# A graph layer with a fixed gather rhythm: a shorter SyncE program, copied pairs from octet 10 on, x held once in SBUF, and another order for the last octets

## The chip, the core and the metric

The kernel runs on one core of one Trainium2 chip. The core has five engines that work side by side, each through its own list of instructions in order: TensorE (PE in the profile; PEld is its load of weights), VectorE (DVE), ScalarE (ACT), GpSimd (POOL) and SyncE (SP), which only issues DMAs and handles registers. The metric is the device time of one execution in microseconds (us), median of several.

## The reference

There are 12500 nodes with 64 features and 400000 edges, sorted by their target node:

```python
m_in = concatenate([x[src], x[dst], edge_attr], axis=-1)      # 400000 x 144
h = silu(m_in @ W1 + b1)
messages = silu(h @ W2 + b2)
agg = segment_sum(messages, dst, num_segments=12500)
out = layernorm(x + silu(concatenate([x, agg], axis=-1) @ W3 + b3))
```

## The kernel before

**Tiles and octets.** 128 edges are a tile, two tiles a pair, eight tiles an *octet*; there are 3125 tiles and 391 octets (the last has five tiles). The 400000 edges are sorted by target, so the targets of an octet lie in a window of 48 nodes that begins at the target of its first edge (`base`). The loop at line 641 runs over the octets `o` and holds the program of PE, ACT, DVE and SP in an order that is written out by hand; POOL's order is the framework's.

**One octet.** The product of the source rows with W1's first part comes from a table `pa` in HBM that the kernel makes in octets 1 to 7 (`table`, L177). From octet 12 on (`RAW`) POOL gathers rows of `pa`, before that rows of x, one indirect DMA of 128 rows for a tile (`gather`, L373, L382), three octets ahead, into five buffers `ga`. `window_load` (L396) has SP bring the x columns of the octet's window, twice, into `xr`; `window_product` (L404) multiplies them by W1's second part, and `window_copy` (L410) masks the result into `xw`. `load` (L413) has SP bring, for three octets, the targets `dr`, twice 48 partitions, and the attributes into `oh`; `compare_dst` (L426) makes one-hot rows of the targets, `compare_nodes` (L436) one-hot columns `eh`. `first_layer` (L443) adds in PSUM the transposed gathered rows (L462) and one product that brings window and attributes (L466); ACT makes h (L469). `second_layer` (L472) follows two octets later (`SECOND`) and gives m (L484), `add_up` (L487) four octets later (`THIRD`) sums by target, and `add_window` (L496) six octets later (`LAST`) adds the window's 48 sums into `agg`. PE's order within an iteration is: window_product of o+1, first_layer of o, add_up of o-4, second_layer of o-2.

**Tiles that POOL doesn't gather.** Two ways take gathers off POOL.

- *Copied pairs* (`pairs`, L271). x lies transposed in SBUF (`xs`), 64 partitions by nodes, and a second time in partitions 64 to 127. For a copied pair ACT and DVE copy the 256 source columns one by one, 64 partitions by 4 bytes, at a place that a register holds (`columns`, L280; L306 on DVE, L308 on ACT): 72 copies per octet on ACT, in parts of 40 and 32, and 64 on DVE, in four parts of 16 (`RATE` is 136). The list of source nodes comes by `index` (L356), is turned into addresses by `address` (L363), and is loaded into registers at most 16 at a time (L299). Such a pair is multiplied on PE (L465). Copies begin in octet 12, and the first copied pair stands in octet 16.
- *Single rows* (`rows`, L321). From octet 12 on SP loads 16 addresses into registers (L329) and issues 16 DMAs of one `pa` row each (L333) per octet; 256 of them make a pair (`rpairs`, 23 of them).

**The nodes.** While the edges run, nodes whose sums are complete pass in groups of 512 through the second product, layernorm and the store (`node_load`, `node_product`, `node_silu`, `node_stats`, `root`, `inverse`, `divide`, `store`, planned by `todo`). The last two groups come at the end (L728 to L742): their product with x and b3 (`node_product(q, 1)`) stands in iteration NO + 1, the product with agg (`part` 2) behind the last add_window. `limits` (L600, with an iota on POOL, L602) and `verdict` (L615) test whether every target lay in its window; if not, a general path runs instead, which this input doesn't need.

Of the kernel before, what the change touches and what calls it, by code (L numbers as in the profile page):

```python
# [20 lines left out]
P = 128  # L21
# [10 lines left out]
RAW = 12  # L32
TABLES = 7
# [4 lines left out]
XBASE = (0, 64 << 18)  # L38
# [9 lines left out]
@with_exitstack  # L48
def kernel(
    ctx: ExitStack,  # L50
    tc: tile.TileContext,
    x: bass.AP,
    xt: bass.AP,
    src_c: bass.AP,
    src_row: bass.AP,
    dst_c: bass.AP,
    dst_row: bass.AP,
    attr_t: bass.AP,
    dst_2: bass.AP,
    attr_2: bass.AP,  # L60
    base: bass.AP,
    w1: bass.AP,
    b1: bass.AP,
    w2: bass.AP,
    b2: bass.AP,
    w3: bass.AP,
    b3: bass.AP,
    out: bass.AP,
    edges: int,
):  # L70

    nc = tc.nc
    N, D = x.shape

    const = ctx.enter_context(tc.tile_pool(name="const", bufs=1))
    dram = ctx.enter_context(tc.tile_pool(name="dram", bufs=1, space=DRAM))
    pa = dram.tile([N, D], F32, name="pa")
    badi = const.tile([1, 1], I32, name="badi")
    ident = const.tile([P, P], F32, name="ident")  # L90
    make_identity(nc, ident)

    with ExitStack() as inner:
        windows(inner, tc, ident, badi, pa, x, xt, src_c, src_row, dst_c, dst_row, attr_t, dst_2, attr_2, base, w1, b1, w2, b2, w3, b3, out, edges)
# [7 lines left out]
def windows(ctx, tc, ident, badi, pa, x, xt, src_c, src_row, dst_c, dst_row, attr_t, dst_2, attr_2, base, w1, b1, w2, b2, w3, b3, out, edges):  # L102
# [46 lines left out]
    resident(0, 0)  # L149
# [3 lines left out]
    resident(0, XC)  # L153
# [47 lines left out]
    nc.gpsimd.iota(coli, pattern=[[0, 1]], base=0, channel_multiplier=1)  # L201
    colf = fast.tile([P, 2], F32, name="colf")
    nc.vector.tensor_copy(colf[:, 0:1], coli)
    nc.vector.tensor_scalar(colf[:, 1:2], colf[:, 0:1], float(S), None, op0=OP.is_ge)
# [5 lines left out]
    nc.vector.tensor_scalar(colf[:, 1:2], colf[:, 1:2], -float(S), None, op0=OP.mult)  # L210
    nc.vector.tensor_tensor(colf[:, 0:1], colf[:, 0:1], colf[:, 1:2], op=OP.add)
# [8 lines left out]
    nc.vector.tensor_copy(wb, pb)  # L220
    nc.vector.tensor_scalar(wn, pb, colf[:, 0:1], None, op0=OP.add)
# [17 lines left out]
    for k in range(3):  # L239
        t = fast.tile([D + 1, 2, S], F32, name=f"xr{k}")  # L240
        nc.vector.memset(t[D:], 1.0)
        xrs.append(t)
# [13 lines left out]
    with tc.tile_pool(name="gat", bufs=AHEAD + 2) as gat, tc.tile_pool(name="drp", bufs=2) as drp, \  # L256
# [23 lines left out]
        def columns(o, eng, part):  # L280
            if o < RAW:
                return
            lo = (o - RAW) * RATE
            if eng == ENG.Activation:
                lo, n = lo + sum(ACOLS[:part]), ACOLS[part]
            else:
                lo, n = lo + sum(ACOLS) + sum(VCOLS[:part]), VCOLS[part]
            hi, todo = lo + n, n
            while lo < hi:
                j, e0 = lo // (2 * P), lo % (2 * P)  # L290
                if j >= len(pairs):
                    return
                n = min(hi - lo, P - e0 % P, LOADS[lo > hi - todo])
                if pairs[j] not in cols:
                    cols[pairs[j]] = cx.tile([P, P], F32, name="cx")
# [3 lines left out]
                _, regs = nc.values_load_multi_w_load_instructions(  # L299
                    indices[j][0:1, e0:e0 + n], engines=(eng,), min_val=XBASE[s] + XADDR,  # L300
                    max_val=XBASE[s] + XADDR + 4 * (N - 1), skip_runtime_bounds_check_because="src names a node")
                for e, r in zip(range(e0 % P, e0 % P + n), regs):
                    to, frm = t[h, 4 * e:4 * e + 4], xb[h, ds(r - (XBASE[s] + XADDR), 4)]
                    if eng == ENG.DVE:

                        nc.vector.tensor_reduce(to, frm[:, :, None], AX.X, OP.max)  # L306
                    else:
                        nc.scalar.copy(to, frm)  # L308
                lo += n
# [8 lines left out]
        single, rindex = {}, {}  # L318
        pab = pa[:, :].bitcast(U8).rearrange("n d -> (n d)")

        def rows(o):  # L321
            lo = (o - RAW) * ROWS
            j, e0 = lo // (2 * P), lo % (2 * P)
            if o < RAW or j >= len(rpairs):
                return
            if e0 == 0:
                single[rpairs[j]] = rx.tile([P, 2, D], F32, name="rx")
            t = single[rpairs[j]].bitcast(U8)
            _, regs = nc.values_load_multi_w_load_instructions(  # L329
                rindex[j][0:1, e0:e0 + ROWS], engines=(ENG.SP,), min_val=0, max_val=4 * D * (N - 1),  # L330
                skip_runtime_bounds_check_because="src names a node")
            for e, r in zip(range(e0, e0 + ROWS), regs):
                nc.sync.dma_start(t[e % P:e % P + 1, e // P, :], pab[ds(r, 4 * D)].rearrange("(o n) -> o n", o=1))  # L333
# [17 lines left out]
        def begun(o):  # L351

            first, behind = -(-(o - RAW) * RATE // (2 * P)), -(-(o + 1 - RAW) * RATE // (2 * P))
# [16 lines left out]
        winrow, winreg = {}, {}  # L370
        sums = psa.tile([P, 4, S], F32, name="pg")
# [15 lines left out]
        def bases(eng, o):  # L387

            n = min(4, NO - o)
            _, regs = nc.values_load_multi_w_load_instructions(  # L390
                bi[0:1, o:o + n], engines=(eng,), min_val=0, max_val=N - 1,
# [4 lines left out]
        def window_load(o):  # L396
# [3 lines left out]
            frm = xt[:, ds(winreg.pop((ENG.SP, o)), S)]  # L400
            nc.sync.dma_start(xr[:D], frm[:, None, :].to_broadcast([D, 2, S]))
            winrow[o] = xr

        def window_product(o):  # L404
            pw = mis.tile([P, P], F32, name="mm")
            nc.tensor.matmul(pw[:E, :], winrow[o].rearrange("k s w -> k (s w)"), w1bb.rearrange("k s m -> k (s m)"),  # L406
# [6 lines left out]
        def load(c, o0=0, o1=CT // OT):  # L413
# [6 lines left out]
            for k in range(2):  # L420
                nc.sync.dma_start(dr[k * S:(k + 1) * S, e], dst_2[k:k + 1, d].to_broadcast([S, e.stop - e.start]))  # L421
# [21 lines left out]
        def first_layer(o):  # L443
# [6 lines left out]
            if o < RAW:  # L450
                nc.tensor.matmul(p1[:, :k], xw[o % 3], oh, start=True, stop=False, skip_group_check=True)
                pt = mis.tile([P, OT // 2, P], F32, name="mm")
                for i in range(k):
                    nc.tensor.transpose(pt[:, i, :], ga[:, 2 * i:2 * i + 2, :].rearrange("p s d -> p (s d)"), ident)
                xg = msg.tile([P, OT // 2, P], F32, name="m")
                nc.vector.tensor_copy(xg[:, :k], pt[:, :k])
                nc.tensor.matmul(p1[:, :k], w1d, xg[:, :k], start=False, stop=True, skip_group_check=True)
# [163 lines left out]

        for o in range(min(AHEAD, NO)):
            gather(o)
# [14 lines left out]
        with tc.manual_schedule(engines={ENG.PE, ENG.Activation, ENG.DVE, ENG.SP}):  # L638
            compare_dst(0)
            compare_nodes(0)  # L640
            for o in range(NO + THIRD):
# [6 lines left out]
                if o < 2:  # L648
                    for c in parts[2:5] if o == 0 else parts[5:]:
                        resident(0, c)  # L650
# [23 lines left out]
                if o + 1 < NO:  # L674
# [3 lines left out]
                if o >= LAST:  # L678
                    add_window(o - LAST)
# [9 lines left out]
                if o + 1 < NO:  # L689
                    window_copy(o + 1)  # L690
# [16 lines left out]
                if o >= THIRD:  # L707
                    add_up(o - THIRD)
                if 0 <= o - SECOND < NO:
                    second_layer(o - SECOND)  # L710
# [6 lines left out]
                if o == NO - 2:  # L717
# [10 lines left out]
        for o in range(NO + THIRD - LAST, NO):  # L728
            add_window(o)
# [4 lines left out]
        for q in range(rest, NG):  # L734
            node_product(q, 2)
            node_silu(q)
            node_stats(q)
        root(rest, NG)
# [261 lines left out]
```

## Time and profile before

| | us |
|---|---|
| median of 3 runs | 3422.63 |
| lowest and highest | 3420.27 and 3425.53 |
| the profiled execution | 3420.95 |
| its span, first to last instruction | 3418.8 |

Busy time in that span: PE 2283.9, PEld 1545.4, DVE 2433.6, ACT 3109.1, POOL 2542.7 us. In the lines of the profile, L382 is line 382 of the kernel; a group's line reads: line, engine, operation, what it writes <- what it reads, count, then busy time in all, mean ns of one, and the idle time of the engine just ahead of it with what ended it. "issue" means that nothing that the profile shows was waited for. A line of the timeline reads: start, duration, engine, line, operation, tiles, count, and in brackets the idle time before it. SPq and ACTq are an engine's issuing of DMAs and its register work. PEclk is the granted share of TensorE's full clock.

### The profile page before, as it was taken

What the parts mean: (1) busy time and instruction counts of PE and PEld (TensorE: products, weight loads), DVE (VectorE), ACT (ScalarE), POOL (GpSimd) and SP (SyncE); (2) the same over time, 40 slices, a digit from 0 to 9 for tenths busy, and PEclk for the clock granted to TensorE, in tenths of its full rate; (3) what the DMA queues carried; (4) which work ended last, traced back from release to release, by engine and by line L of the source; (5) the groups of instructions that cost most, each with busy time, mean ns of one, the idle gap of its engine ahead of it and who ended that gap; (6) DMA issues with size and microseconds to landing.
All of it is one profiled execution on the core that took longest, in us unless ns stands there. A gap on an engine that the chain in (4) does not pass through costs nothing. (4 is left out here: it accounts for less than half of the span.)

```text
span 3418.8 us, 107012 instructions
## 1 busy us (share of the span) xinstructions
PE 2283.9 (67%) x13764; PEld 1545.4 (45%) x13764; DVE 2433.6 (71%) x26003; ACT 3109.1 (91%) x27413; POOL 2542.7 (74%) x2696
## 2 busy tenths in 40 slices
PE   6777776666666666666666656666667576666667
PEld 4545444444444444444444444434444354444444
DVE  2577777677776777778777777777787776877772
ACT  2499999999999999999999999998999999999992
POOL 7777777777777777777777777776777777777774
PEclk7756566676666777677676667776766766777766
DMA  6532233233333322323332233233223223332322
GB/s 136 119 64 61 62 65 65 62 63 67 69 61 65 66 61 63 68 60 66 72 62 59 62 69 60 62 69 66 62 61 68 61 61 69 65 62 60 69 60 58
DMA packets 202928, 229.05 MB, mean 67 GB/s; under 512 B 133023, under 2 KB 141413, under 8 KB 201301
## 3 DMA queue, kind: packets, MB, share of 16 engines
q1 hardware_dynamic: 101560, 122.63, 16.1%
q0 software_dynamic: 85984, 88.22, 13.8%
q10 hardware_dynamic: 14652, 11.26, 1.5%
q14 instruction: 615, 5.03, 0.5%
q8 instruction: 117, 1.92, 0.2%
HBM read 215.45 MB, written 6.40 MB: 65 GB/s over the span
## 5 line engine op out<-in xcount | busy, mean ns | idle before, releaser
L382 POOL DMA_INDIRECT ga<-pa,sc x2591 | 2449.8, 945 | 813.4 <-issue 702.5
L308 ACT COPY cx<-xs 64x4 uint8 x26568 | 2646.4, 187 | 60.7 <-issue 37.2
L306 DVE TENSOR_REDUCE cx<-xs 64x4 uint8 x23608 | 1684.2, 153 | 527.3 <-issue 477.2
L406 PE MATMUL mm<-w1bb,xr 65*96 65x128 f32 x782 | 234.6, 395 | 839.2 <-DMA xr<-in_xt 673.6
L466 PE MATMUL p<-oh,xw 128*128 128x512 f32 (+1 forms) x758 | 601.7, 890 | 0.0
L480 PE MATMUL p<-w2d,h 128*128 128x128 f32 x3126 | 571.7, 339 | 0.0
L406 PEld LDWEIGHTS mm<-w1bb,xr 65*96 65x96 f32 x782 | 141.0, 226 | 890.3 <-DMA xr<-in_xt 785.1
L493 PEld LDWEIGHTS pg<-eh,m 128*64 128x64 f32 x6250 | 283.0, 175 | 574.6 <-issue 368.2
L480 PEld LDWEIGHTS p<-w2d,h 128*128 128x128 f32 x3126 | 483.1, 236 | 114.7 <-issue 114.7
L493 PE MATMUL pg<-eh,m 128*64 128x48 f32 x6250 | 334.8, 263 | 104.8 <-DVE agg L498 101.8
L433 DVE TENSOR_TENSOR oh<-dr,wrow 96x512 f32<-96x512 int32 x391 | 263.6, 674 | 150.4 <-DMA dr<-in_dst 70.8
L462 PE MATMUL p<-ident,ga 128*128 128x128 f32 x1296 | 318.9, 372 | 68.4 <-DMA ga<-pa,sc 68.1
L469 ACT ACTIVATE h<-p 128x512 f32<-128x512 f32 x391 | 231.7, 592 | 144.8 <-PE p L466 99.9
L462 PEld LDWEIGHTS p<-ident,ga 128*128 128x128 f32 x1296 | 236.1, 196 | 84.6 <-issue 80.3
L484 ACT ACTIVATE m<-p 128x512 f32<-128x512 f32 x391 | 231.4, 592 | 43.5 <-PE p L480 31.2
L439 DVE TENSOR_TENSOR eh<-wrow,dc 128x384 f32<-128x384 f32 x391 | 214.3, 548 | 2.7
L498 DVE TENSOR_TENSOR agg<-agg,pg 128x48 f32 x391 | 78.2, 200 | 188.3 <-PE mm L533 113.3
L466 PEld LDWEIGHTS p<-oh,xw 128*128 128x128 f32 x758 | 179.6, 291 | 0.0
L478 PE MATMUL p<-b2r,one 3*128 3x512 bf16 x391 | 177.5, 454 | 0.0
L411 DVE TENSOR_TENSOR xw<-mm,mask 96x128 f32<-96x128 f32 x391 | 109.6, 280 | 23.1 <-PE mm L406 15.2
L382 POOL DMA_INDIRECT ga<-in_x,sc x96 | 90.8, 946 | 30.2 <-issue 28.0
L465 PE MATMUL p<-cx,w1d 128*128 128x128 f32 x392 | 109.9, 377 | 0.0
(84 smaller groups left out, 780.2 us busy)
## 6 DMA issues: line engine op xcount, KB each, us to landing
rx<-pa SPq DMA_DIRECT2D x5888, 0.2 KB
dr<-in_dst SPq DMA_DIRECT2D x260, 288.0 KB
ga<-pa,sc POOLq DMA_INDIRECT x2591
oh<-in_attr SPq DMA_DIRECT2D x130, 192.0 KB
xr<-in_xt SPq DMA_DIRECT2D x391, 24.0 KB
xs<-in_xt ACTq DMA_DIRECT2D x12, 512.0 KB
cxi<-in_src_row SPq DMA_DIRECT2D x196, 1.0 KB
pa<-v ACTq DMA_DIRECT2D x12, 256.0 KB
```

The lines of the kernel that those rows point to most:

```text
L306: nc.vector.tensor_reduce(to, frm[:, :, None], AX.X, OP.max)
L308: nc.scalar.copy(to, frm)
L382: nc.gpsimd.indirect_dma_start(out=ga[:, i, :], out_offset=None, in_=x if o < RAW else pa[:, :], in_offset=bass.IndirectOffsetOnAxis(ap=sc ...
L406: nc.tensor.matmul(pw[:E, :], winrow[o].rearrange("k s w -> k (s w)"), w1bb.rearrange("k s m -> k (s m)"), start=True, stop=True)
L433: nc.vector.tensor_tensor(oh[:E, :], dr[:, e:e + w], wn[:E, o:o + 1].to_broadcast([E, w]), op=OP.is_equal)
L439: nc.vector.tensor_tensor(eh[:, :n], row[:, None, :].to_broadcast([P, n, S]), rel[:, t0:t0 + n, None].to_broadcast([P, n, S]), op=OP.is_equal)
L462: nc.tensor.matmul(p1[:, i, :], g2.rearrange("p s d -> p (s d)"), ident, is_transpose=True, start=(i == c), stop=False, skip_group_check=True)
L466: nc.tensor.matmul(p1[:, :k], xw[o % 3], oh, start=False, stop=True, skip_group_check=True)
L469: nc.scalar.activation(h[:, :k], p1[:, :k], AF.Silu)
L480: nc.tensor.matmul(p2[:, 2 * i:2 * i + 2, :].rearrange("p s d -> p (s d)"), h[:, i, :], w2d, start=False, stop=(i == k - 1), skip_group_ch ...
L484: nc.scalar.activation(m[:, :n2], p2[:, :n2], AF.Silu)
L493: nc.tensor.matmul(pg[s * D:(s + 1) * D, :], m[:, i, :], eh[:, i, :], start=(i < 2), stop=(i >= n - 2), skip_group_check=True)
```

## The change

- **Slices from doubled columns.** A new array `xt2` holds every column of x's transpose twice in a row. The window's slice is one run of 384 bytes in each of 64 partitions, in place of two of 192. So rows and columns of the two tiles of a pair alternate in `dr`, `mask`, `colf` and `wn` (partition 2w + tile in place of 48 tile + w). The registers of `base` are loaded for SP from a copy times 8 (`bi8`), so that the byte offset needs no step of its own.
- **One DMA for `dr`** in place of two.
- **32 registers at a time** for the single rows, in every second octet.
- **Copies from octet 6 on** (`BEGIN`): copied pairs begin in octet 10.
- **x once.** `xs` is filled in partitions 0 to 63 only; copies for the second tile of a pair read there and write partitions 64 to 127. `address` is one instruction for both tiles.
- **The last octets.** second_layer of the last three octets comes one octet after first_layer; add_up of the last three after two octets and of the three before after three; add_window after 3, 4, 4 and 5. The last window product is made an octet earlier. The two last node groups' first products move from iteration NO + 1 to NO - 3 and NO - 2, `limits` and `verdict` behind the loop, the statistics behind both second products.

```diff
+BEGIN = 6
-XBASE = (0, 64 << 18)
...
-    def resident(s, c):
+    def resident(c):
         w = min(XC, NP - c)
-        nc.scalar.dma_start(xs[s * D:(s + 1) * D, c:c + w], xt[:, c:c + w])
+        nc.scalar.dma_start(xs[:D, c:c + w], xt[:, c:c + w])
...
     nc.vector.tensor_copy(wb, pb)
+    bi8 = bf.bitcast(I32)
+    nc.vector.tensor_scalar(bi8, bi, 8.0, None, op0=OP.mult)
...
-            o = RAW + -(-2 * P * (len(pairs) + 1) // RATE) + 2
+            o = BEGIN + -(-2 * P * (len(pairs) + 1) // RATE) + 2
...
-                    to, frm = t[h, 4 * e:4 * e + 4], xb[h, ds(r - (XBASE[s] + XADDR), 4)]
+                    to, frm = t[h, 4 * e:4 * e + 4], xb[:D, ds(r - XADDR, 4)]
...
-            _, regs = nc.values_load_multi_w_load_instructions(
-                rindex[j][0:1, e0:e0 + ROWS], engines=(ENG.SP,), min_val=0, max_val=4 * D * (N - 1),
-                skip_runtime_bounds_check_because="src names a node")
-            for e, r in zip(range(e0, e0 + ROWS), regs):
+            if o % 2 == 0:
+                _, rowreg[:] = nc.values_load_multi_w_load_instructions(
+                    rindex[j][0:1, e0:e0 + 2 * ROWS], engines=(ENG.SP,), min_val=0, max_val=4 * D * (N - 1),
+                    skip_runtime_bounds_check_because="src names a node")
+            for e in range(e0, e0 + ROWS):
+                r = rowreg.pop(0)
...
-                t = indices[j]
-                for s in range(2):
-                    h = slice(s * P, (s + 1) * P)
-                    nc.vector.tensor_scalar(t[:, h], t[:, h], 4.0, float(XBASE[s] + XADDR), op0=OP.mult, op1=OP.add)
+                nc.vector.tensor_scalar(indices[j], indices[j], 4.0, float(XADDR), op0=OP.mult, op1=OP.add)
...
-            frm = xt[:, ds(winreg.pop((ENG.SP, o)), S)]
-            nc.sync.dma_start(xr[:D], frm[:, None, :].to_broadcast([D, 2, S]))
+            nc.sync.dma_start(xr[:D, :].bitcast(U8), xt2b[:, ds(winreg.pop((ENG.SP, o)), 8 * S)])
...
-            for k in range(2):
-                nc.sync.dma_start(dr[k * S:(k + 1) * S, e], dst_2[k:k + 1, d].to_broadcast([S, e.stop - e.start]))
+            nc.sync.dma_start(dr[:, e], dst_2[None, :, d].to_broadcast([S, 2, e.stop - e.start]))
...
+        seconds = times({None: SECOND, 0: 1, 1: 1, 2: 1})
+        adds = times({None: THIRD, 0: 2, 1: 2, 2: 2, 3: 3, 4: 3, 5: 3})
+        folds = times({None: LAST, 0: 3, 1: 4, 2: 4, 3: 5})
...
-                if 5 <= o < 5 + (len(parts) + 1) // 2:
-                    for c in parts[(o - 5) * 2:(o - 4) * 2]:
-                        resident(1, c)
...
-                if o == NO - 1:
-                    bad = limits()
-                if o == NO + 1:
-                    verdict(bad)
-                    for q in range(rest, NG):
+                if o == NO - 3:
+                    node_product(rest, 1)
+                if o == NO - 2:
+                    for q in range(rest + 1, NG):
                         node_product(q, 1)
```

More of the change, by code (lines that the diff above doesn't have):

```diff
@@ L280, in columns @@
         def columns(o, eng, part):
-            if o < RAW:
+            if o < BEGIN:
                 return
-            lo = (o - RAW) * RATE
+            lo = (o - BEGIN) * RATE
             if eng == ENG.Activation:
@@ L351, in begun @@
         def begun(o):
-            first, behind = -(-(o - RAW) * RATE // (2 * P)), -(-(o + 1 - RAW) * RATE // (2 * P))
+            first, behind = -(-(o - BEGIN) * RATE // (2 * P)), -(-(o + 1 - BEGIN) * RATE // (2 * P))
             return range(max(0, first), max(0, min(behind, len(pairs))))
@@ L389, in bases @@
             n = min(4, NO - o)
+            at, unit = (bi8, 8) if eng == ENG.SP else (bi, 1)
             _, regs = nc.values_load_multi_w_load_instructions(
-                bi[0:1, o:o + n], engines=(eng,), min_val=0, max_val=N - 1,
+                at[0:1, o:o + n], engines=(eng,), min_val=0, max_val=unit * (N - 1),
                 skip_runtime_bounds_check_because="dst names a node")
@@ L405, in window_product @@
             pw = mis.tile([P, P], F32, name="mm")
-            nc.tensor.matmul(pw[:E, :], winrow[o].rearrange("k s w -> k (s w)"), w1bb.rearrange("k s m -> k (s m)"),
+            nc.tensor.matmul(pw[:E, :], winrow[o], w1bb.rearrange("k s m -> k (s m)"),
                              start=True, stop=True)
@@ L450, in first_layer @@
             if o < RAW:
+                c = 1 if o in pairs else 0
                 nc.tensor.matmul(p1[:, :k], xw[o % 3], oh, start=True, stop=False, skip_group_check=True)
+                if c:
+                    nc.tensor.matmul(p1[:, 0, :], w1d, cols.pop(o), start=False, stop=False, skip_group_check=True)
                 pt = mis.tile([P, OT // 2, P], F32, name="mm")
-                for i in range(k):
+                for i in range(c, k):
                     nc.tensor.transpose(pt[:, i, :], ga[:, 2 * i:2 * i + 2, :].rearrange("p s d -> p (s d)"), ident)
                 xg = msg.tile([P, OT // 2, P], F32, name="m")
-                nc.vector.tensor_copy(xg[:, :k], pt[:, :k])
-                nc.tensor.matmul(p1[:, :k], w1d, xg[:, :k], start=False, stop=True, skip_group_check=True)
+                nc.vector.tensor_copy(xg[:, c:k], pt[:, c:k])
+                nc.tensor.matmul(p1[:, c:k], w1d, xg[:, c:k], start=False, stop=True, skip_group_check=True)
             else:
@@ L620, in verdict, with times @@
             nc.vector.tensor_copy(badi, bs)
+        def times(lags):
+            at = {}
+            for o in range(NO):
+                at.setdefault(o + lags.get(NO - 1 - o, lags[None]), []).append(o)
+            return at
+        seconds = times({None: SECOND, 0: 1, 1: 1, 2: 1})
+        adds = times({None: THIRD, 0: 2, 1: 2, 2: 2, 3: 3, 4: 3, 5: 3})
+        folds = times({None: LAST, 0: 3, 1: 4, 2: 4, 3: 5})
         for o in range(min(AHEAD, NO)):
@@ L640, in windows @@
             compare_nodes(0)
-            for o in range(NO + THIRD):
+            for o in range(NO + 2):
                 if o == 0:
@@ L677, in windows @@
                     bases(ENG.DVE, o - 4)
-                if o >= LAST:
-                    add_window(o - LAST)
+                for q in folds.get(o, []):
+                    add_window(q)
                 if o + 1 < NO:
@@ L706, in windows @@
                         table(c)
[L707 to L710, printed above, removed]
+                for q in adds.get(o, []):
+                    add_up(q)
+                for q in seconds.get(o, []):
+                    second_layer(q)
                 address(o + 2)
@@ L736, in windows @@
             node_silu(q)
+        for q in range(rest, NG):
             node_stats(q)
+        verdict(bad)
         root(rest, NG)
```

45 lines of the change are left out of this document (27 added, 18 removed).

## The prediction

> **What bounds the kernel now.** I read the page first for its busy shares and its costliest groups, then the table by stretches, then the waits of POOL and of SP, and last the timelines of SP and of the ending.
>
> ```profile
> span 3418.8 us, 107012 instructions
> L382 POOL DMA_INDIRECT ga<-pa,sc x2591 | 2449.8, 945 | 813.4 <-issue 702.5
> L308 ACT COPY cx<-xs 64x4 uint8 x26568 | 2646.4, 187 | 60.7 <-issue 37.2
> L306 DVE TENSOR_REDUCE cx<-xs 64x4 uint8 x23608 | 1684.2, 153 | 527.3 <-issue 477.2
> ```
> ```profile
> 1000.00:2000.00 1000.00, 649.21 (x3990) 443.20 (x3990) 738.56 (x8058) 957.03 (x8561) 755.54 (x801) 0.70 0.31 64
> 2000.00:3000.00 1000.00, 659.35 (x4017) 444.87 (x4015) 745.35 (x8110) 960.40 (x8577) 746.12 (x789) 0.70 0.31 64
> 3000.00:3300.00 300.00, 185.07 (x1177) 125.64 (x1176) 217.69 (x2383) 284.05 (x2546) 221.30 (x234) 0.70 0.31 64
> 3300.00:3350.00 50.00, 41.47 (x250) 29.44 (x249) 31.02 (x278) 41.19 (x326) 36.13 (x39) 0.67 0.40 84
> ```
>
> In the second fence the columns are stretch, length, busy time and count of PE, PEld, DVE, ACT and POOL, then clock, DMA share and GB/s. ACT has the largest share, yet POOL ends the kernel: between 1000 and 2000 us it issued 801 gathers, one per 1000/801 = 1.2484 us (945 ns and an issue gap of 0.30), without a hole. The other 2000 us are no such clean run: 789 gathers in the next 1000 us are 1000 - 789 x 1.2484 = 15.0 us short, 234 in the next 300 are 7.9 short, 39 in the next 50 are 1.3 short. So **24.2 us** of POOL time are lost after 2000 us, and almost none before.
>
> ```profile
> POOL ga L382 <- PE p L462: 3.6, 10, 0.8
> POOL ga L382 <- PE p L462: 30.1, 24, 3.8
> ```
>
> These are the waits of POOL on the transposes that free a `ga` buffer, from 1000 to 2000 us (total, times, longest) and from 2000 us on. So the consumer of the gathers falls behind slowly and has used up its cushion by 2000 us. Its pace follows from the second stretch, where POOL is its slave: an octet takes 8 - 2 x 136/256 - 2 x 16/256 = 6.8125 gathers, so 789 gathers are 115.8 octets, 8.63 us each. POOL alone would take 6.8125 x 1.2484 = **8.505 us**. Who sets 8.63?
>
> ```profile
> 2314.99 0.61 SPq L401 DMA_DIRECT2D xr<-in_xt  x1
> 2317.21 5.52 SPq L333 DMA_DIRECT2D rx<-pa  x16
> ...
> 2323.30 0.66 SPq L401 DMA_DIRECT2D xr<-in_xt  x1
> 2325.53 5.09 SPq L333 DMA_DIRECT2D rx<-pa  x16
> 2330.72 0.79 SPq L421 DMA_DIRECT2D dr<-in_dst  x2
> 2331.61 0.69 SPq L422 DMA_DIRECT2D oh<-in_attr  x1
> 2332.48 0.61 SPq L401 DMA_DIRECT2D xr<-in_xt  x1
> 2334.66 5.44 SPq L333 DMA_DIRECT2D rx<-pa  x16
> ...
> 2341.64 0.61 SPq L401 DMA_DIRECT2D xr<-in_xt  x1
> ```
> ```profile
> 2337.35 0.74 PE L406 MATMUL mm<-w1bb,xr 65*96 65x128 f32 x2 [5.99 <-DMA xr<-in_xt]
> ```
> ```profile
> SPq L333 <- DMA oh<-in_attr: 20.2, 50, 1.3
> ```
>
> SP does. The slice `xr` is issued once per octet; three octets take 2341.64 - 2314.99 = 26.65 us, 8.88 each (this stretch also holds a list of rows and a load of four registers that not every octet has), and what stands between the rows is register work, not waiting: the third fence is the longest entry in SP's list of waits from 1000 to 3000 us, 20.2 us of 2000. PE meets the slice late (5.99 us idle in this octet), and first_layer stands behind that product. The other engines have room at 8.63 us per octet: ACT 960.40/115.8 = 8.29, DVE 745.35/115.8 = 6.44 and some 477.2/379 = 1.3 of issue, PE 5.7.
>
> **The change part by part.** *Three more pairs.* With BEGIN = 6 the recurrence in `pairs` gives 199 pairs in place of 196, and each takes two gathers off POOL: 6 x 1.2484 = **7.5 us**, on the path. The 768 copies more are worked in octets 6 to 11, which had few:
>
> ```profile
> 80.00:100.00 20.00, 18.30 (x100) 13.35 (x100) 3.50 (x8) 3.57 (x7) 15.13 (x17) 0.74 0.90 185
> 100.00:120.00 20.00, 17.44 (x147) 11.80 (x145) 6.44 (x16) 4.90 (x9) 15.12 (x17) 1.00 0.88 200
> ```
> ```profile
> 81.59 0.94 POOL L382 DMA_INDIRECT ga<-in_x,sc  x1 [0.30 <-issue]
> ```
> ```profile
> 107.79 0.60 ACT L469 ACTIVATE h<-p 128x512 f32<-128x512 f32 x1 [2.90 <-PE p L457]
> ...
> 130.45 0.60 ACT L469 ACTIVATE h<-p 128x512 f32<-128x512 f32 x1 [2.96 <-PE p L457]
> ```
>
> Per octet ACT gets 72 x 2646.4/26568 = 7.2 us, DVE 64 x 1684.2/23608 = 4.6 and about 1.3 of issue. An octet of eight gathers is 10 us of POOL, so in 20 us ACT rises from 3.6 to 4.9 to about 18 to 19, DVE to about 15 to 18: it fits, but the catching up goes. Today the eighth h (107.79) comes 25.3 us after its octet's last gather (the 64th, ended at 82.53), and the twelfth (130.45) 8 us after the 96th gather, which by the pitch ends at 122.5. With ACT at 8.3 to 8.5 us per octet from octet 6 on the lag stays near 25. POOL waits when octet o-5 is not yet read, that is, above four octets or 34 us. About 9 us of cushion are left, and at 8.3 against 8.505 the lag shrinks from there. I take nothing for it; if ACT's pace is over 8.505, the price is the first rival.
>
> *SP.* The rows of its instructions (ns: shortest/median/longest):
>
> ```profile
> L329 SPq TENSOR_LOAD <-rxi x368: 972/1415/1439, 129.1 to 3327.2; - x184
> ```
> ```profile
> L401 SPq ALU_OP  x391: 32/41/54, 8.3 to 3358.9; - x196
> ...
> L401 SPq DMA_DIRECT2D xr<-in_xt x391: 598/615/1432, 8.5 to 3359.0; - x196
> ```
> ```profile
> L421 SPq DMA_DIRECT2D dr<-in_dst x264: 311/408/1577, 9.3 to 3356.3; - x132
> ```
> ```profile
> L390 SPq TENSOR_LOAD <-bi x98: 302/557/914, 7.7 to 3349.8; - x98
> ```
> ```profile
> L333 SPq DMA_DIRECT2D rx<-pa x5888: 224/225/352, 130.7 to 3334.1; - x197
> ```
>
> No row shows the new forms, so each has two ends. The slice loses its ALU step (0.04) and goes from 64 x 2 runs to 64: at most 0.615 as now, at least 0.225 as one row; I take 0.41, as a `dr` of 48 rows, saving 0.2. One `dr` for two: 0.41 to 0.82; I take 0.6, saving 0.2 per three octets. The load of 32 registers for two of 16: four cost 0.557 and sixteen 1.415, 0.0715 for each more, so 32 cost 2.56 and save 0.27 per two octets; ends: 1.415 (nothing for the added registers) and 2.83 (no saving). With the dispatch of the dropped instructions the sum is 0.04 + 0.2 + 0.07 + 0.13 + about 0.05 = 0.5 us per octet; the least end is under 0.1, the most 1.2. SP goes from 8.63 to about 8.1, under POOL's 8.505, and the **24.2 us** of waits go. The least end would leave it at 8.55.
> The Trainium skill, "DMA: Bandwidth & Descriptors", section "Latency and other measured facts", puts a floor of about 600 ns under a tensor_load; by it one load fewer per two octets would save 0.3 us per octet, and the sum be 0.65. The row of four registers (557) agrees, but its shortest, 302, does not.
>
> *x once.* The second half of xs is no longer loaded; copies for a pair's second tile read partitions 0 to 63 and write 64 to 127. The load itself lay beside POOL: 0. For the crossing no row exists; I take 0, since the copy moves 4 bytes in each of 64 partitions as before, and the other end is the second rival. `address` is one instruction for two, on DVE, off the path. The one wait that is added in the start is SP's first load of bases: it reads `bi8`, which DVE writes behind this copy.
>
> ```profile
> 5.04 0.57 DVE L220 COPY wb<-mm 128x391 f32<-128x391 f32 x1 [1.01 <-PE mm L219]
> ```
>
> So it is there before 7.7, when SP comes to the load; the slices and `dr` queued behind it on SP are not late. Cost 0, and POOL, 25 us ahead by octet 7, would cover some us.
>
> *The ending.*
>
> ```profile
> 3369.39 1.23 POOL L602 IOTA xs<- 128x393 int32 x1
> ...
> 3385.79 1.06 POOL L382 DMA_INDIRECT ga<-pa,sc  x1 [0.30 <-issue]
> ```
> ```profile
> 3388.63 1.49 PE L466 MATMUL p<-oh,xw 128*128 128x384 f32 x2
> ...
> 3396.35 0.69 PE L528 MATMUL mm<-b3r,ones 1*128 1x256 f32 x2
> ...
> 3399.03 1.09 PE L528 MATMUL mm<-b3r,ones 1*53 1x256 f32 x2
> ...
> 3401.08 1.09 PE L493 MATMUL pg<-eh,m 128*64 128x48 f32 x16
> ...
> 3403.95 3.17 PE L533 MATMUL mm<-w3s,agg 128*128 128x64 f32 x16 [0.54 <-DVE agg L498]
> ```
>
> The iota keeps its place 13 gathers before the end. From the last gather's end (3386.85) to the span's end are 31.95 us. PE works with hardly a hole from the last first_layer to L533. The change moves the first node product (3399.03 - 3396.35 = 2.7) and one add_up (1.1) ahead of the last gathers, where PE waits for data; the second product, another second layer and add_up come between the last two first_layers, where PE has no hole, so they only change places. Against this, lags of one octet show the wait for m (0.6 and two hand-overs, about 0.85) twice, and `bs` now stands in DVE ahead of the statistics and waits for the verdict's matmul, about 0.6. Sum: -2.7 - 1.1 + 1.7 + 0.6 = **-1.5 us**, with ends of -4 (the waits hidden) and +2.5 (the moved work delays the last first_layer).
>
> Sum against the profiled execution's own 3420.95 us: -7.5 - 24.2 - 1.5 = -33.2, 3387.8. That execution is 1.7 below the median of the runs shown, 3422.63; I give **3388**.
>
> **The rivals.**
> 1. *A pace remains.* SP's least end, or ACT with its in-order waits, leaves 8.55 per octet instead of 8.505. The start's lag of 25 leaves 9 us of cushion, used after 9/0.045 = 200 octets; the 170 left cost 0.045 each, 8 us: 3396; at 8.6 it is 95 octets and 273 x 0.095 = 26 us: 3414. For it: ACT's 957 of 1000. Against: ACT's 8.29 holds all of its work.
> 2. *Crossing copies do not overlap* (slower). Copies now follow each other at 71 ns on DVE and 99.6 on ACT, though one lasts 153 and 187. If a copy that reads one half and writes the other waits for the one before it, 32 on DVE cost 82 more (2.6 us) and 36 on ACT 87 more (3.1 us) per octet. ACT then needs 11.4, and 377 octets x 2.9 less the cushion give about 4450 us. It decides from (8.505 - 8.29 + 0.09)/36 = 8 ns per copy on. Nothing before shows such a copy. The Trainium skill, "VectorE: DVE Perf Modes", section "Two Vector instructions with no wait between them", holds a Vector instruction when its input's start quadrant differs from the preceding input's, or its output's from the preceding output's; by that rule a run of crossing copies is not held, and the time stays 3388. No row bears on it; it lowers this rival for me.
> 3. *The waits were not SP's.* If POOL's holes stay, only 9 us are gained: 3412; with the dear end of the ending 3416. Against: PE's idle time names `xr`.
>
> **How the numbers follow.** Forecast 0.72 (3380 to 3394 by the ends of the ending and 2 to 3 us of small holes); rival 1 0.13, of which 0.02 is a pace above 8.6, beyond 3416; rival 3 0.06, of which 0.02 comes with the dear ending; rival 2 0.05; a pace of 8.66 (by rival 1's working 9/0.155 = 58 octets, then 310 x 0.155 = 48 us: 3436) 0.02; under 3380 0.02. A measurement of this kernel can tell about 0.2%, 7 us, from no change. Faster: 0.72 + 0.11 + 0.04 + 0.02 = 0.89; within: 0.02 + 0.02 = 0.04; slower: 0.05 + 0.02 = 0.07. The range 3380 to 3402 takes in the forecast and most of rival 1.
>
> **What would show it.** Right: 2587 gathers from pa and 94 from x, one per 1.248 us to the end, POOL's waits on L462's counterpart near nothing; SP with waits of its own; PE's wait on `xr` mostly gone; h lagging the gathers by about 25 us near octet 10, less later; copies at 71 and 99.6 ns apart. Wrong: a copy group's busy time per copy grown (rival 2), holes in POOL beside a full ACT or SP (rival 1), a last gather to end of more than 34 us.

## The result and the profile after

Changed kernel: 3394.93 us (median of 4 runs, 3393.94 to 3397.24), beside 3424.08 for the kernel before (4 runs, 3420.27 to 3430.72). The ratio is 0.9914, 95% interval 0.9897 to 0.9931: **about 29 us faster**. The forecast was 3388, the range 3380 to 3402. The profiled executions are 3420.95 and 3397.24 us, with spans of 3418.8 and 3395.5.

First the page of the changed kernel, then its table by stretches (columns as in the prediction), then POOL's waits on the transposes from 1000 to 2000 us and from 2000 us on.

```profile
span 3395.5 us, 106488 instructions
L385 POOL DMA_INDIRECT ga<-pa,sc x2587 | 2446.3, 946 | 790.0 <-issue 705.5
L311 ACT COPY cx<-xs 64x4 uint8 x27000 | 2700.5, 189 | 37.8 <-issue 22.3
L309 DVE TENSOR_REDUCE cx<-xs 64x4 uint8 x23944 | 1670.6, 140 | 542.6 <-issue 497.0
...
L385 POOL DMA_INDIRECT ga<-in_x,sc x94 | 88.9, 945 | 30.3 <-issue 26.5
```
```profile
1000.00:2000.00 1000.00, 660.07 (x4055) 448.05 (x4053) 736.68 (x8167) 967.32 (x8695) 756.33 (x800) 0.70 0.30 65
2000.00:3000.00 1000.00, 666.75 (x4076) 453.18 (x4076) 738.06 (x8132) 972.72 (x8724) 755.72 (x802) 0.71 0.29 66
3000.00:3300.00 300.00, 202.82 (x1270) 138.95 (x1270) 214.64 (x2319) 288.60 (x2559) 226.83 (x241) 0.70 0.30 67
3300.00:3350.00 50.00, 8.03 (x56) 5.73 (x55) 5.18 (x15) 2.03 (x4) 38.26 (x41) 0.56 0.15 30
```
```profile
POOL ga L385 <- PE p L467: 3.1, 10, 0.3
POOL ga L385 <- PE p L467: 2.4, 8, 0.3
```

POOL now issues 802 gathers from 2000 to 3000 us, where it issued 789, and 241 from 3000 to 3300, where it issued 234. Its 30.1 us of waits on the transposes after 2000 us are 2.4. The copies, half of which now cross the halves, stand 2700.5/27000 = 100.0 ns and 1670.6/23944 = 69.8 ns apart.

The last row is new. From 3300 to 3350 us POOL gathers on, while ACT has 2.03 us of work in 50 and DVE 5.18. The timeline of DVE in the changed kernel shows why, below it that of ACT, then the iota on POOL and PE's first row after the stop:

```profile
3297.35 0.97 DVE L568 TENSOR_SCALAR v<-v,mv,rstd 128x64 f32<-128x64 f32 x4
3341.70 0.57 DVE L609 TENSOR_TENSOR xs<-xs,wb 128x391 f32<-128x391 int32 x1 [43.38 <-POOL xs L607]
```
```profile
3303.45 0.60 ACT L474 ACTIVATE h<-p 128x512 f32<-128x512 f32 x1 [2.70 <-PE p L471]
3347.54 0.60 ACT L489 ACTIVATE m<-p 128x512 f32<-128x512 f32 x1 [43.49 <-PE p L485]
...
3374.64 0.49 ACT L474 ACTIVATE h<-p 128x384 f32<-128x384 f32 x1 [1.96 <-PE p L471]
```
```profile
3340.43 1.24 POOL L607 IOTA xs<- 128x393 int32 x1
```
```profile
3343.81 1.09 PE L498 MATMUL pg<-eh,m 128*64 128x48 f32 x16 [40.45 <-DVE agg L503]
```

DVE stands for 43.38 us on the iota of `limits()` (L607), which POOL reaches only at 3340.43, 13 gathers before its end. Behind that instruction stand `oh`, `xw` and `eh` of the last octets, so PE, ACT and SP stand too. Six h are still to be made when DVE is released; they come at 3.5 us each or slower, and the last one starts 16.5 us after the last gather's end (3.4 before).

| us | before | changed | difference | predicted |
|---|---|---|---|---|
| gathers at 1.2484 | 2687 | 2681 | -7.5 | -7.5 |
| POOL's time above that pitch, from its first gather on (holes, iota) | 29.6 | 8.5 | -21.2 | -24.2 |
| last gather ends | 3386.84 | 3358.12 | -28.7 | -31.7 |
| from there to the last h | 3.4 | 16.5 | +13.1 | |
| from there to the span's end | 28.6 | 20.8 | -7.7 | |
| last gather to end, the last two together | 31.9 | 37.3 | **+5.4** | **-1.5** |

So the stream came nearly as forecast, and the ending is the step that failed. From 2000 us on the time above the pitch fell from 26.4 to 1.9 us, 24.5 us as against the 24.2 forecast; the 3 us that lack are holes before 2000 us, 6.9 in place of 3.6 (3.0 in another execution of the changed kernel, `changed_third` below). The two drains (what follows the last gather) did not run at one clock: the granted clock was 0.76 and then 0.58 before, 0.93 and then 0.86 in the changed kernel, so the slower clock lies in the shorter drain, and +5.4 is no measure of the ending at like clocks.

### The profile page after: what moved, and what is told of

Its sections match the earlier page's. It is cut to its first block, busy times and chain, and to the rows that moved or that the text cites. A ratio compares the mean times of both kernels' runs of the same rounds, so it can differ in the third digit from the quotient of the medians.

```text
span 3395.5 us, 106488 instructions
## 1 busy us (share of the span) xinstructions
PE 2249.9 (66%) x13767; PEld 1536.8 (45%) x13767; DVE 2406.7 (71%) x26146; ACT 3136.8 (92%) x27845; POOL 2537.3 (75%) x2690
## 5 line engine op out<-in xcount | busy, mean ns | idle before, releaser
L311 ACT COPY cx<-xs 64x4 uint8 x27000 | 2700.5, 189 | 37.8 <-issue 22.3
L309 DVE TENSOR_REDUCE cx<-xs 64x4 uint8 x23944 | 1670.6, 140 | 542.6 <-issue 497.0
L471 PE MATMUL p<-oh,xw 128*128 128x512 f32 (+1 forms) x758 | 580.6, 860 | 0.0
L485 PE MATMUL p<-w2d,h 128*128 128x128 f32 x3126 | 571.3, 339 | 0.0
L485 PEld LDWEIGHTS p<-w2d,h 128*128 128x128 f32 x3126 | 482.5, 236 | 115.3 <-issue 115.3
L498 PE MATMUL pg<-eh,m 128*64 128x48 f32 x6250 | 327.9, 260 | 185.4 <-DVE agg L503 166.6
L467 PE MATMUL p<-ident,ga 128*128 128x128 f32 x1294 | 298.1, 362 | 1.5 <-DMA ga<-pa,sc 1.5
L471 PEld LDWEIGHTS p<-oh,xw 128*128 128x128 f32 x758 | 172.7, 280 | 0.0
L414 DVE TENSOR_TENSOR xw<-mm,mask 96x128 f32<-96x128 f32 x391 | 109.5, 280 | 22.1 <-PE mm L409 16.3
```

The source lines that it names most:

```text
L467: nc.tensor.matmul(p1[:, i, :], g2.rearrange("p s d -> p (s d)"), ident, is_transpose=True, start=(i == c), stop=False, skip_group_check=True)
L471: nc.tensor.matmul(p1[:, :k], xw[o % 3], oh, start=False, stop=True, skip_group_check=True)
L485: nc.tensor.matmul(p2[:, 2 * i:2 * i + 2, :].rearrange("p s d -> p (s d)"), h[:, i, :], w2d, start=False, stop=(i == k - 1), skip_group_ch ...
L498: nc.tensor.matmul(pg[s * D:(s + 1) * D, :], m[:, i, :], eh[:, i, :], start=(i < 2), stop=(i >= n - 2), skip_group_check=True)
```

## The experiments

Ratios are to the kernel before, run beside each.

**1. `limits()` back in the loop.**

In the changed kernel the call stands behind the hand-written order; here it stands inside it again, as in the kernel before.

```diff
+                if o == NO - 1:
+                    bad = limits()
...
-        bad = limits()
```

> The changed kernel with limits() back inside the loop at o == NO - 1, nothing else. In the changed kernel DVE stood 43.4 us on the iota of limits() (from 3298.3 to 3341.7), and PE, ACT and SP behind it; the last h came 16.5 us after the last gather (3.4 before the change) and the span ended 20.9 us after that h. Theory (DVE's wait lengthened the drain): no such wait, the last h 3 to 5 us after the last gather, a drain of 24 to 31 us in place of 37.4, so 3382 to 3389 us. Rival (the new lags and node products themselves make the drain long): the drain stays at 36 to 38 us and the time at 3394 to 3396.

Measured: 3385.42 us (5 runs, 3383.90 to 3389.64), ratio 0.9904 (0.9886 to 0.9921). The last gather of its profile ends at 3356.68, the last h starts 6.1 us later (3 to 5 expected), and the drain is 26.85. DVE's timeline in this kernel:

```profile
3355.18 0.20 DVE L503 TENSOR_TENSOR agg<-agg,pg 128x48 f32 x1 [8.89 <-PE pg L498]
3355.30 0.56 DVE L609 TENSOR_TENSOR xs<-xs,wb 128x391 f32<-128x391 int32 x1
```

The subtraction stands behind the last `eh`, and waits for nothing. The drain is as the theory has it, and what it lost lay wholly ahead of the last h (the stretch behind it is 20.8 us in both kernels). The clock is not the reason: it was 0.81 and then 0.86 here, lower than the changed kernel's 0.93 and 0.86. The times alone don't decide it, since the two kernels ran on different occasions and their ratios overlap (0.9914 with 0.9897 to 0.9931 for the changed one); experiment 3 runs such a pair side by side.

**2. The old order of the last octets as a whole**, with `limits()` in its old place (lags 2, 4 and 6, node products two octets behind the end; the diff of the change's last hunks turned back).

> The changed kernel with the whole old order of the last octets (lags 2, 4 and 6, limits() at o == NO - 1, node products two octets behind the end). Theory (DVE's wait on the iota, which the new place of limits() brought): the last gather ends near 3358 as in the changed kernel and the drain is the 32 us of before, 3389 to 3391 us, so the new ending cost about 5 us. Rival (a leaner stream brings more work to the end, whatever the order): drain of 36 or more and 3394 to 3396.

Measured: 3387.57 us (5 runs, 3385.60 to 3391.00), ratio 0.9906 (0.9889 to 0.9923). That is 2 us above `limits_in_loop`, which ran beside it, and by the ratios it can't be told apart from that kernel or from the changed one. The time is 1.4 us under the range of the theory. In the profile the last gather ends at 3353.96, not near 3358, and the drain is 35.25 us, not 32. The windows from the last gather on say why; first this kernel, then `sp_alone` (experiment 5), which has the same ending and a drain of 29.27, and then one row of PE's timeline of each:

```profile
3354.00:3362.00 8.00, 7.96 (x52) 5.44 (x51) 0.39 (x2) 1.69 (x3) 0.00 (x0) 0.50 0.02 4
3362.00:3372.00 10.00, 10.00 (x50) 7.32 (x50) 0.51 (x4) 1.09 (x2) 0.00 (x0) 0.50 0.01 3
```
```profile
3363.30:3371.00 7.70, 7.68 (x77) 5.44 (x76) 0.41 (x2) 2.22 (x4) 0.00 (x0) 0.82 0.03 6
3371.00:3378.00 7.00, 6.60 (x51) 5.29 (x51) 0.69 (x4) 0.55 (x2) 0.00 (x0) 0.88 0.01 2
```
```profile
3358.67 2.08 PE L485 MATMUL p<-w2d,h 128*128 128x128 f32 x8
```
```profile
3367.20 1.16 PE L485 MATMUL p<-w2d,h 128*128 128x128 f32 x8
```

The granted clock is 0.50 in one and 0.82 to 0.88 in the other, and eight matmuls of L485 take 2.08 us or 1.16. PE is busy through nearly all of these stretches, so one profiled drain is good to some 6 us only. Against the rival (a leaner stream brings more work to the end) speaks the 29.27 of `sp_alone`, whose stream has as few holes. At like clocks (0.82 to 0.88 here, 0.81 to 0.86 in `limits_in_loop`) the new ending without the stop saves 29.27 - 26.85 = 2.4 us, by one pair of profiles.

**3. The changed kernel and a repaired one side by side.** The repaired one moves `limits()` as in 1, its iota to the start of POOL's order, and the subtraction and reduction that read the iota to octet 28, so that only small comparisons are left at the end:

```diff
+        evi = xs.bitcast(I32)[D:, :3 * NCH]
+        nc.gpsimd.iota(evi, pattern=[[STEP, NCH], [0, 3]], base=0, channel_multiplier=0)
...
         for o in range(min(AHEAD, NO)):
             gather(o)
...
+                if o == 28:
+                    lag = xs[D:, 3 * NCH:3 * NCH + NO]
+                    nc.vector.tensor_tensor(lag, evi[:, :NO], wb[D:], op=OP.subtract)
+                    nc.vector.tensor_reduce(lim[D:, 2:3], lag, AX.X, OP.max)
```

> The changed kernel itself, as the partner of the next one. Theory (DVE's wait of 43 us on the iota costs the drain about 10 us): last h 14 to 19 us after the last gather, drain 35 to 39 us, and a median 8 to 13 us above that of iota_early_b. Rival (the chip and the clock made the 10 us between the changed kernel and limits_in_loop): within 3 us of it. On a chip where all kernels take 5500 us, as in the runs before, neither can be told.

> The kernel of iota_early once more: limits() in the loop at o == NO - 1, the iota at the start of POOL's order in the free half of xs, the lag's reduction (on 64 partitions that hold the same values) in octet 28. Theory: no wait of DVE on the iota, last h 3 to 7 us after the last gather, drain of 24 to 29 us, and 1.2 us of POOL's time less than limits_in_loop: last gather at 3352 to 3356, 3380 to 3387 us. Rival: as changed_third within 3 us.

Measured: changed 3396.33 us (6 runs, 3395.02 to 3398.95), ratio 0.9933 (0.9912 to 0.9953); repaired 3383.72 (5 runs, 3382.11 to 3388.36), ratio 0.9897 (0.9873 to 0.9920). That is **12.6 us** between them, and the ranges lie apart. DVE's stop in the changed kernel is there again, longer:

```profile
DVE xs L609 <- POOL xs L607: 47.4, 1, 47.4
```

Its drain is 37.47 us, the repaired one's 24.87; the last h starts 16.5 and 4.1 us after the last gather. The repaired kernel has the lowest median of all that were run. That its iota comes early brought nothing that can be seen, though 1.2 us were expected: it ends at 2.78 and delays the first gather by about 0.2 us, and the last gather ends at 3356.56 (3352 to 3356 expected), in the changed kernel beside it at 3356.26. POOL's time above the pitch differs by 2 us between the two executions of the changed kernel (8.5 and 6.5), more than the iota takes. So the 12.6 us lie in the drain, where DVE's stop is.

**4. All of SP's edits undone.** Slice from `xt` twice with its ALU step, two `dr` DMAs, 16 registers at a time; everything else as changed. The slice's columns and the rows of `dr` then stand in the old order and `mask` and `wn` in the new one, so the columns that the one-hot picks are not the reference's; instructions and shapes are those of the theory.

> The changed kernel with SP's three edits undone (slice from xt twice with its ALU step, two dr DMAs, 16 registers at a time); x once, BEGIN = 6 and the new ending stay. Theory (SP paces the consumer at 8.63 us per octet): with a start lag of 35 us, the cushion is gone by octet 13, and 375 octets x (8.63 - 8.505) = 47 us of POOL's time go, in place of 8.2: last gather near 3397, about 3425 to 3440 us. Rival (POOL's holes of before had another cause, which the rest of the change took away): holes as in the changed kernel, 3393 to 3400.

Measured: 3433.0 us (8 runs, 3424.18 to 3439.39), ratio 1.0039 (1.0025 to 1.0053); POOL's time above the pitch is 47.1 us, and its waits on the transposes from 1000 us on:

```profile
POOL ga L380 <- PE p L463: 50.4, 37, 5.8
```

Without SP's edits the change makes the kernel slower: **SP set the pace**. The size was right (47 expected), but by luck, since the place was not: the lag of h behind the gathers stays at 22 to 28 us up to octet 85, and the holes come from 1000 us (octet 110) on. Some 280 octets lost 0.16 us each, where 375 of 0.125 were expected.

**5. SP's edits and x once alone**: `BEGIN = 12` and the old ending.

> The changed kernel with BEGIN = 12 and the old ending: what is left of the change is SP's three edits and x once. Theory: 2687 gathers without holes but for 1 to 3 us: 2.7 + 2687 x 1.2484 + 3 = 3360 for the last one, 32 us of drain, so 3390 to 3394 us, 28 to 33 below the kernel before; against the changed kernel's stream the three pairs then bring only about 2 us net, since 7.5 saved stand against some 6 us of holes in its octets 12 to 20. Rival (SP's edits save too little): holes from 2000 us on remain and the time lies at 3400 to 3421.

Measured: 3395.76 us (4 runs), ratio 0.9932 (0.9912 to 0.9952). The last gather ends at 3363.26, with 6.1 us above the pitch, and the time is 1.8 us over the expected range. Against `old_ending`, on the same chip and differing only in BEGIN, it is 8.2 us slower. My expectation of 2 us for the three pairs fails, and the prediction's 7.5 stands: the last gathers lie 9.3 us apart.

**6. One SP edit at a time**, each on the kernel before with x once (one DMA for `dr` alone was not run). First the slice alone, with the two `dr` DMAs on every second partition, as the doubled columns want it:

```diff
-            frm = xt[:, ds(winreg.pop((ENG.SP, o)), S)]
-            nc.sync.dma_start(xr[:D], frm[:, None, :].to_broadcast([D, 2, S]))
+            nc.sync.dma_start(xr[:D, :].bitcast(U8), xt2b[:, ds(winreg.pop((ENG.SP, o)), 8 * S)])
```

> The kernel before with x once and, of SP's edits, only the slice from doubled columns (two dr DMAs and loads of 16 registers stay; rows of dr interleaved as the doubled columns want it). Theory (SP paces the consumer; by the rows of the changed kernel the slice saves 0.626 + 0.041 + 0.042 - 0.497 = 0.21 us per octet, 8.63 to 8.42, under POOL's 8.505): POOL's holes after 2000 us shrink from 23 to under 4 us, 20 to 26 us less than before. Rival (only all three edits together are enough): more than 10 us of holes remain.

Measured: 3395.73 us (4 runs), ratio 0.9928 (0.9901 to 0.9955), 2.1 us of holes from 2000 to 3300 us (23.2 before). The slice alone takes the holes away: POOL issues 801 gathers from 2000 to 3000 us (first row), where the next kernel, with the load of 32 registers alone, issues 788 (second row).

```profile
2000.00:3000.00 1000.00, 656.81 (x4060) 446.84 (x4060) 733.89 (x8086) 967.28 (x8672) 756.02 (x801) 0.70 0.26 65
```
```profile
2000.00:3000.00 1000.00, 653.91 (x4016) 442.24 (x4015) 727.25 (x8024) 954.39 (x8560) 744.14 (x788) 0.70 0.29 64
```

The edit of that next kernel:

```diff
-            _, regs = nc.values_load_multi_w_load_instructions(
-                rindex[j][0:1, e0:e0 + ROWS], ...
+            if o % 2 == 0:
+                _, rowreg[:] = nc.values_load_multi_w_load_instructions(
+                    rindex[j][0:1, e0:e0 + 2 * ROWS], ...
```

> The kernel before with x once and, of SP's edits, only the load of 32 registers for two octets. Theory: by the rows 2 x (1.306 + 0.053) - (2.309 + 0.057) = 0.35 us per two octets, 0.18 per octet, 8.63 to 8.45, under POOL's 8.505: holes after 2000 us under 6 us, 17 to 25 us less than before. Rival (two octets' rows in one block after a load of 2.3 us make the slice of every second octet late): holes of 10 us or more remain.

Measured: 3420.25 us (10 runs), ratio 1.0001 (0.9986 to 1.0015), 22.1 us of holes from 2000 to 3300 us: nothing, although the load does take 2.31 us in place of two of 1.41. The expectation fails, and the holes are those of its rival. SP's waits from 1000 to 3000 us in this kernel:

```profile
SPq L336 <- DMA dr<-in_dst: 36.3, 48, 1.6
SPq L336 <- DMA oh<-in_attr: 21.1, 35, 1.3
...
SPq L336 <- DMA xr<-in_xt: 4.5, 11, 0.9
```

They are 61.9 us, where the kernel before has 20.2 + 8.4 + 6.1 = 34.7: the row DMAs now wait for the landing of `dr` and `oh`. Over the 230 slices issued in that time it is 0.12 us per octet of the 0.18 saved; the row DMAs' issues, 235 ns on the mean in place of 230, take another 0.08. That both come from issuing a row DMA soon after the last ones is my reading, and the rival's reason (a late slice in every second octet) was not tested apart from it; that SP's pace did not move is shown.

**7. x once alone, and three runs beside it, on a slower chip.**

> The kernel before with x once in SBUF and nothing else of the change: copies for a pair's second tile read partitions 0 to 63 and write 64 to 127. Theory (a copy that crosses the halves overlaps its neighbours as any other): 70 ns apart on DVE and 100 on ACT, POOL's holes of 25 to 33 us as before, a time within 0.2% of the kernel before. Rival (crossing copies wait for one another): 150 ns and 190 ns apart for half of them and a time of 4300 us or more.

> The changed kernel itself, beside the two that follow on one chip. Theory (DVE's wait on the iota costs the drain about 10 us): last h 14 to 18 us after the last gather and a drain of 35 to 39, and a median 7 to 12 us above that of limits_again. Rival (the 10 us between the earlier runs were the chip's and the clock's): within 3 us of limits_again.

> The kernel of limits_in_loop once more, as the partner of changed_again. Theory: drain of 25 to 30 us, last h 3 to 7 us after the last gather, 3382 to 3388 us. Rival: as changed_again within 3 us.

> limits_in_loop with its iota, a copy of the lag and the lag's reduction moved: the iota goes to the start of POOL's order, into the half of xs (partitions 64 to 127) that the change left free, and DVE reduces it in octet 28; the last octets keep only three small comparisons. The check of the lag then reads 64 partitions, which all hold the same values. Theory (POOL is the bound to its last gather, so an iota among the last gathers costs its own time): 1.2 us less for the last gather than in limits_again, and 0.5 to 2 us less in all. Rival (POOL's time before the first gather is not free): the first gather begins 1 us later, at 3.8, and nothing is gained.

All four, and the kernel before (5518.86 us), took 1.6 times as long on this chip: x once 5501.41 (ratio 0.9969, 0.9958 to 0.9981), changed 5495.01 (0.9962, 0.9948 to 0.9975), `limits_again` 5496.48 (0.9960, 0.9946 to 0.9973), `iota_early` 5495.00 (0.9963, 0.9950 to 0.9977). The page of `limits_again`:

```profile
L311 ACT COPY cx<-xs 64x4 uint8 x27000 | 2914.0, 189 | 1734.4 <-issue 1707.2
L385 POOL DMA_INDIRECT ga<-pa,sc x2587 | 2447.5, 946 | 2848.7 <-PE p L467 1883.2
```

Durations are the old ones (189 and 946 ns), but ACT has 1707.2 us of "issue" before its copies (20.9 in `limits_in_loop`), and POOL waits 1883.2 us for the transposes. Neither POOL's gathers nor the ending is the bound there, and the expectations on the ending fail: the drain of `limits_again` is 44.60 us (25 to 30 expected), longer than the 39.02 of `changed_again`. So the three runs of other endings tell nothing of the ending; the changed kernel and `iota_early` were run again in experiment 3. What the fourth does tell: with crossing copies the kernel is no slower here either. It is 0.3% faster, where at most 0.2% either way was expected; why was not looked into.

## Why the prediction was right, and where not

- *POOL's gathers bound the stream, one per 1.2484 us*: right. 802 gathers in a full 1000 us.
- *Three more pairs, 7.5 us*: right (experiment 5), and the cushion held. The lag near octet 10, forecast as 25, was 35.3 us in the profiled execution, 21.1 in `changed_third` and 25.7 in `limits_in_loop`, which start alike. Even the longest left room: PE had read octet 8's rows at 125.49, and POOL took their buffer for octet 13 at 129.62. In the first of the three POOL also waited once for the table, at octet 12; the other two show no such hole, so its cause stays open.

```profile
122.13 0.94 POOL L385 DMA_INDIRECT ga<-pa,sc  x1 [1.53 <-DMA pa<-v]
```
- *SP sets 8.63 us per octet, so its waits go*: right in cause (experiment 4) and effect (30.1 us to 2.4), wrong in size. The sum was 0.5 us per octet; SP's slices from 1000 to 3000 us are 236 in place of 231, from the first to the last 8.50 us apart in place of 8.65, that is **0.15**. POOL was not what held SP at that: from octet 130 to 340 the lag of h behind the gathers is 18.6 us on the mean, in place of the 4 us of octets 13 to 15 of the kernel before, where PE waits for the gathers. Rows of the changed kernel:

```profile
L333 SPq TENSOR_LOAD <-rxi x184: 2287/2309/2335, 166.8 to 3269.2; - x184
```
```profile
L404 SPq DMA_DIRECT2D xr<-in_xt x391: 468/495/1181, 8.5 to 3353.7; - x196
```
```profile
L423 SPq DMA_DIRECT2D dr<-in_dst x132: 573/634/654, 9.1 to 3350.0; - x132
```
```profile
L424 SPq DMA_DIRECT2D oh<-in_attr x132: 316/542/1817, 9.8 to 3353.2; - x132
```
```profile
SPq L338 <- DMA dr<-in_dst: 56.9, 44, 3.1
SPq L338 <- DMA oh<-in_attr: 21.8, 43, 1.5
...
SPq L338 <- DMA xr<-in_xt: 7.1, 13, 1.2
```

  By medians the slice saves 0.615 - 0.495 = 0.12 (0.2 forecast) besides the ALU step's 0.08 with its gap. `dr` takes 0.634 (0.6 forecast), which saves 2 x 0.408 - 0.634 = 0.18 per three octets, and the `oh` DMA behind it, not edited, now takes 0.542 in place of 0.367 and gives it back. The load takes 2.31 (2.56 forecast), 0.52 less per two octets by the medians. Against these stand waits for landings of 85.8 us in place of 34.7, 0.2 per octet, and dearer row issues. So the sign "SP with waits of its own" came, but SP waits mostly for its own earlier DMAs, not for room. The slice alone was enough: POOL needs 8.505, and in `only_xr` SP issued 234 slices, 8.54 us apart; 380 octets x 0.03 is 11 us, less than the cushion of 34. The forecast of this step was saved by a threshold, not by its sum, and that is luck.
- *PE's wait on `xr` mostly gone*: wrong. It was 542.4 us before on PE's weight loads from 1000 to 3000 us and is 525.9 (299.2 in `changed_third`, 389.3 in `limits_in_loop`):

```profile
PEld mm L409 <- DMA xr<-in_xt: 525.9, 135, 10.6
```

  PE waits for the slice whenever it is ahead of SP, also where POOL is never held up. It was no sign of what the time hangs on; POOL's waits were.
- *Crossing copies cost nothing* (rival 2 refuted): right, 100.0 and 69.8 ns apart, 99.6 and 71 before. By the Trainium skill, "VectorE: DVE Perf Modes", section "Two Vector instructions with no wait between them", a run of them isn't held; the trace agrees with 69.8 ns, though one copy lasts 140.
- *The load of registers.* One load in place of two saved 2 x 1415 - 2309 = 521 ns, but SP's pace did not move (experiment 6), so nothing hung on it. The Trainium skill, "DMA: Bandwidth & Descriptors", section "Latency and other measured facts", gives a `tensor_load` a floor of about 600 ns; this case's loads go under it, since four registers took 302 ns at the shortest and 557 at the median (L390 of the kernel before).
- *The ending, -1.5 us with ends of -4 and +2.5*: **wrong, +5.4**. The step that failed is "The iota keeps its place 13 gathers before the end". It does, on POOL. But the subtraction that reads it, on DVE, did not keep its own: with `limits()` behind the hand-written order, the scheduler put it ahead of the compares of the last six octets. The prediction priced `bs` and the lags and never asked where the other instructions of `limits()` went, nor what would queue behind a DVE that waits for POOL. The price is the 10.4 to 12.4 us by which the last h came late (16.5 us after the last gather, 6.1 and 4.1 without the stop). The prediction's own sign of being wrong, more than 34 us from the last gather to the end, came with 37.3. The rest of that sum was sound: the two waits for m are 0.75 and 0.64 (0.85 each forecast), and without the stop the ending saves 2.4 at like clocks.

Without the stop the forecast of 3388 would have been close: 3385.42 and 3383.72. The measured 3394.93 lies in the stated range by luck: its upper part was kept for a pace of SP that remains (rival 1), not for a stop in the ending.

## What to carry to other kernels

When code is moved out of a hand-written order, look up where each of its instructions lands on each engine, and for each that waits, what stands behind it; one small check that waited held four engines here. Near a threshold a small saving does all of the work and the next ones none: ask by how much the slower stage is over the faster one, before adding up savings. And time saved between DMA issues can come back as waits for earlier ones to land.

## What was not expected of the hardware

- The issue time of a DMA on SP depends on its neighbours: `oh`, unchanged, took 0.367 us behind two `dr` of 48 rows and 0.542 behind one of 96 (0.536 behind two of 48 whose rows lie on every second partition, which took 0.580 each in place of 0.408).
- 4, 16 and 32 registers took 0.557, 1.415 and 2.309 us to load: the second sixteen cost 0.056 each, the twelve before them 0.0715.
- The clock granted in the last 30 us was 0.50 in some executions and 0.8 in others, and the same ending's drain was 29.3 us at 0.82 to 0.88 and 35.3 us at 0.50 (36.2 and 35.1 in `only_xr` and `only_regs`, also at 0.50).
- On one chip every kernel took 1.6 times as long, with idle time on ACT that no wait explains. Single instructions of ACT and POOL lasted as long as elsewhere (189 and 946 ns); the granted clock was lower, 0.59 in place of 0.70, and a matmul of L485 took 382 ns in place of 348, which makes 0.1 ms over its 3126 matmuls where 2.1 ms are lost. What held the engines there stays open.
